# An edge-gated graph layer on one core: the weighted copy of a part taken over into the next part, and the hot edges' W2 products put ahead of the hot tiles' products

## The chip, the core and the metric

The kernel runs on one core of a Trainium2 chip. The metric is device time in microseconds (us), the median of several executions. One further execution was taken with the hardware profiler; all rows of a profile come from it. The engines are called TensorE (PE in the rows; PEld is its weight load), VectorE (DVE), ScalarE (ACT), GpSimd (POOL) and SyncE (SP, which issues DMAs here).

## The reference

There are 12,500 nodes with 128 features and 412,500 edges (each drawn edge in both directions, and a loop for each node), sorted by destination. All is float32.

```
theta = x[dst] - x[src]
w     = sigmoid(relu(theta @ W1 + b1) @ W2 + b2)          # one number per edge
agg   = segment_sum(w * theta, dst)
indeg = segment_sum(1, dst)
out   = layernorm(x + agg + indeg * (x @ W4 + b4))
```

## The kernel before, in words

**Preparation.** A table z is written to DRAM that holds for each node the rows `x @ W1` and x side by side, so that one gather by source brings both. The first 18 parts (`PLAIN`) are handled by `early_part`, which the change doesn't touch.

**Parts and blocks.** The other edges are cut into parts of 1532 consecutive edges (`CE`). Two parts make a block of destinations (`SUB = 2`): an even part (h = 0) begins the block b, an odd one (h = 1) ends it. `part(s)` (L1459) writes down the work of one part in the program's order, for s from 18 up to the last part and a few beyond. TensorE, VectorE and ScalarE are under a manual schedule: each runs its instructions in the order in which `part` calls them. What one engine needs from another is waited for by semaphores that the framework inserts.

**Ordinary edges.** Up to 1024 edges of a part are gathered, 128 by each of eight indirect DMAs on GpSimd (`gather`, L398), three parts ahead. TensorE spreads the destinations' rows to the edges by one-hot products (`spread_y`, L885, two parts ahead, into one of two PSUM banks called y). VectorE subtracts the gathered rows (L943), applies relu and W2 (L948), sums to the logits `lg` (L954) and compares indices to make the one-hots `ow` (`one_hot_w`, L918); L918 comes ahead of L954 in even parts and behind it in odd ones. ScalarE makes the gate, a sigmoid of `lg`: once into the PSUM tile `fix` (`open_gate`, L960) and once into the row buffer `wx` (`gate_sums`, L966). Then the gathered x rows are multiplied by the gate into `wx`: four of the eight slots by VectorE (`weigh`, L988, the weighted copy), four by ScalarE (`weigh_rest`, L995). In the next part TensorE sums `wx` by destination (`begin_block` in an odd part, `add_block` in an even one, both L1130).

**Hot edges.** Up to 512 other edges of a part (`HK`) have sources in small ranges of nodes that are kept on chip (`tabs`), so they are not gathered but fetched by one-hot products. ScalarE makes the one-hots `of` of one set of tiles in a part (`hot_tiles` L1033 and L1035, called by `fetch_step` at the end of a part), TensorE multiplies in the next part (`products_of_tiles`, `hot_products`, L1049, 16 products), and ScalarE copies the result to `xT` in the part after that (`hot_out`, L1063). One part ahead of their sums, the hot edges of part t = s + 1 go through `hot_turned` (L1076 and L1077, into the bank `pz`), `hot_relu` (ScalarE, L1082), `hot_rows` (L1090: the W2 products, four of them, into `fix`; L1093: four transposes of xT into `pz`) and `hot_weights` (ScalarE: L1099 sigmoid, L1102 four weighted evictions of `pz`). `one_hot_h` (VectorE, L1112) makes their destinations' one-hots `owh` once a block, in the even part.

**The shared bank.** `fix` is one PSUM bank that holds an index row (read by L918 and L1112), W2 (read by L948), the hot edges' logits (written by L1090, read by L1099), the gates (written by L960, read by L988) and the block's own rows (`own`, written by L1205, read and written by L1223).

**Ends of blocks.** In an odd part the block before is ended: `total` (L1184), `finish` (L1195), `own` (L1203, L1205), and on VectorE `normalize` (L1223 to L1248). `shift` (L1124, L1125) makes the matrix that carries sums over from block to block.

**Placing of the edge lists.** A generator `place` sorts the next 64 parts' edge lists into hot and ordinary slots, mainly on VectorE (32 rounds of L576, L580, L583 a list, and others) with some steps on ScalarE and TensorE. It is advanced in small steps by `spend`, which has a credit of 2.5 a part, so that a part holds about 3 us of it until a list is done. There are five lists; the last four are placed during the stage of `part`.

Of the kernel before, what the change touches and what calls it, by code (L numbers as in the profile page):

```python
# [44 lines left out]
PLAIN = FIRST + MORE  # L45
# [37 lines left out]
def gnn_resnorm(  # L83
# [41 lines left out]
    NS = PLAIN - (E1 - E) // CE  # L125
    NF = PLAIN + (E - E1) // CE
    TAIL = E - E1 - (NF - PLAIN) * CE
    NK = NS // SUB
# [9 lines left out]
    while n0 < N:  # L138
        t = max(1, (N - n0) // P)
# [231 lines left out]
    def filled(t, s):  # L371

        if s < NF:
            return t
        return t.rearrange("p (h j) d -> p h j d", h=2)[:, :, :JT, :]

    def wx_of(s):

        if s < NH:
            return wxe_buf[s % 2]  # L380
        return wx_buf[s % (EW if s < PLAIN else NW)]

    def rows_of(s):

        if s < NH:
            t = zbuf[s // 2].rearrange("p k d -> p (k d)")[:, (s % 2) * BE:(s % 2 + 1) * BE]
            return t.rearrange("p (k d) -> p k d", d=D)
        return zbuf[(s - NH + NX) % NZ]
# [322 lines left out]
    with tc.manual_schedule(engines={SP}), tc.tile_pool(name="work", bufs=2) as wp, tc.tile_pool(  # L711
# [143 lines left out]
        def one_hot(b, c0=0, c1=RW):  # L855

            at = (b - PLAIN // SUB) % NO * RW
            oh = oh_all[:, at:at + RW]
            blocks[b]["oh"] = oh
            if not c0:  # L860
                for i in range(SUB):
                    parts[b * SUB + i] = {"oh": oh}
            oh = oh[:, c0:c1]
            nc.scalar.activation(oh, blocks[b]["to_all"][:, c0:c1], AF.Abs, scale=mine, bias=away)
            nc.scalar.activation(oh, oh, AF.Relu, scale=-1.0, bias=1.0)  # L865
# [106 lines left out]
        def weigh(s):  # L972

            zs = rows_of(s)
            if s < PLAIN:
                wx = wx_of(s)
                for k in range(K):
                    nc.scalar.activation(wx[:, k, :D], zs[:, k, :] if s < NH else zs[:, k, D:],
                                         AF.Copy, scale=wx[:, k, D:D + 1])
                return  # L980
            w = gate[:, s % 2].rearrange("p (k e) -> p k e", e=1)
            wx = wx_of(s)[:, :, :D]
            if s < NF:
                xs = zs[:, :KV, D:]
                w, wx = w[:, :KV], wx[:, :KV]
            else:
                xs, w, wx = filled(zs[:, :, D:], s), filled(w, s), filled(wx, s)
            nc.vector.tensor_tensor(wx, xs, w.to_broadcast(list(xs.shape)), op=OP.mult)  # L988

        def weigh_rest(s):  # L990

            if s < NF:
                wx = wx_of(s)
                for k in range(KV, K):
                    nc.scalar.activation(wx[:, k, :D], rows_of(s)[:, k, D:], AF.Copy,  # L995
                                         scale=wx[:, k, D:D + 1])
# [87 lines left out]
        def hot_rows(t):  # L1084

            xT = xT_all[:, (t - PLAIN) % HX, :]
            hr = parts[t]["hr"]
            for q in range(HQ):
                at = slice(q * P, (q + 1) * P)
                nc.tensor.matmul(lgh[:, t % SUB, q:q + 1], hr[:, at], w2_c, start=True, stop=True)  # L1090
            for q in range(HQ):
                at = slice(q * P, (q + 1) * P)
                newest[0] = nc.tensor.transpose(pz[:, at], xT[:, at], ident)  # L1093

        def hot_weights(t):

            b, h = divmod(t, SUB)
            wx = wxh_buf[b % len(wxh_buf)][:, h * HQ:(h + 1) * HQ, :]
            nc.scalar.activation(wx[:, :, D:D + 1], lgh[:, h].rearrange("p (q e) -> p q e", e=1),  # L1099
                                 AF.Sigmoid, bias=b2_c)  # L1100
            for q in range(HQ):
                nc.scalar.activation(wx[:, q, :D], pz[:, q * P:(q + 1) * P], AF.Copy,  # L1102
                                     scale=wx[:, q, D:D + 1])
# [13 lines left out]
        def shift(b):  # L1117

            sh = blocks[b]["sh"] = wp.tile([P, WB], F32, name="sh")
            if b * SUB < PLAIN:  # L1120
                nc.vector.tensor_scalar(sh[:WB, :WB], lag[:WB, :WB], step_c[:WB, b:b + 1],
                                        None, op0=OP.is_equal)
                return
            nc.scalar.activation(sh[:WB, :WB], lag[:WB, :WB], AF.Abs, scale=-1.0, bias=step_c[:WB, b:b + 1])  # L1124
            nc.scalar.activation(sh[:WB, :WB], sh[:WB, :WB], AF.Relu, scale=-1.0, bias=1.0)  # L1125
# [71 lines left out]
        def own(b):  # L1197

            d = blocks[b]
            a = d["a"]  # L1200
            plain = b * SUB < PLAIN
            sw = wp.tile([P, 2], F32, name="sw")
            nc.scalar.activation(sw[:WB], a[:WB, D:AW], AF.Copy, bias=1.0)  # L1203
            d["own"] = d["xw"][:WB] if plain else own_f[:WB]
            nc.scalar.activation(d["own"], d["xw"][:WB], AF.Copy, scale=sw[:WB, 0:1])  # L1205
            d["deg"] = a[:WB, D + 1:AW] if plain else sw[:WB, 1:]
# [45 lines left out]
        def fetch(b):  # L1252
            if b < NK:
                load_block(b)
# [32 lines left out]
        def advance(kinds, n=1):  # L1287

            for _ in range(n):
                if steps[0] is None or steps[1] not in kinds:  # L1290
                    return
                steps[1] = next(steps[0], None)
                if steps[1] is None:
                    steps[0] = None
# [8 lines left out]
        def tiles_of(group):  # L1303

            x = 0
            for f in group:
                hot_tiles(f, x)
                tiled.append((f, x))
                x += (f[2] - f[0]) * EP
# [9 lines left out]
        def fetch_step(s):  # L1319

            for f in rest_of:
                if f[0] - 4 == s:
                    tiles_of([f])
# [4 lines left out]
        def spend(kinds, most=NS):  # L1328

            while most and credit[0] > 0 and steps[0] is not None and steps[1] in kinds:  # L1330
                credit[0] -= cost[steps[1]]
                advance(kinds)
                most -= 1
# [117 lines left out]
        def spread_ahead(s):  # L1451

            if s + 2 < NS:
                spread_y(s + 2)
                if PLAIN + AHEAD <= s + 3 < NS:
                    paced[s + 3] = newest[0]
                    gather(s + 3)

        def part(s):  # L1459

            b, h = divmod(s, SUB)
            t = s + 1
            credit[0] = min(credit[0] + 2.5, 5.0)
            if s in turns:
                edges[s + 3] = turns[s], load(turns[s])
            if s in edges:
                i, loaded = edges.pop(s)
                assert steps[0] is None
                steps[:] = place(i, lambda: where[0](), *loaded), "k"
            for f in rest_of:  # L1470
                if f[0] - 7 == s:
                    hot_load(f)
            if h == 0:
                fetch(b + 2)
            if s == PLAIN:
                normalize(b - 2)
            done_b = h == 1 and PLAIN // SUB - 1 <= b - 1 < NK
            if t < NS:
                hot_turned(t)
            while opened:  # L1480
                hot_out(*opened.pop(0))
            if t < NS:
                hot_relu(t)
            if done_b:
                total(b - 1)
            advance("c")
            if s < NS:
                logits(s)
            if done_b:
                finish(b - 1)  # L1490
            spread_ahead(s)
            if tiled:
                products_of_tiles()
            if t < NS:
                hot_rows(t)
            if h == 0 and PLAIN // SUB <= b - 1 < NK:
                add_block(b - 1)
            if h == 1 and b < NK:
                begin_block(b)
            if h == 0 and b + 1 < NK:  # L1500
                one_hot(b + 1, BP, RW)
            if h == 1 and b + 2 < NK:
                one_hot(b + 2, 0, BP)
            if t < NS:
                hot_weights(t)
            if s < NS:
                open_gate(s)
                if h == 0:
                    one_hot_h(b)
                else:  # L1510
                    shift(b)
                    spend("kz", 1)
                weigh(s)
                gate_sums(s)
            if done_b:
                own(b - 1)
            if s < NS:
                weigh_rest(s)
            spend("kspmz")
            if done_b:  # L1520
                normalize(b - 1)
            fetch_step(s)

        with tc.manual_schedule(engines=IN_ORDER):
            for s in range(PLAIN, NS + 4):
# [201 lines left out]
```

## Time and profile before

| | us |
|---|---|
| median of 3 executions | 3545.08 (3541.45 to 3546.11) |
| the profiled execution | 3547.81 |
| its span, first to last instruction | 3545.8 |
| stage of `part`, from the first L943 to the last | 302.2 to 3522.5 |
| busy TensorE, weight loads | 2803.1 (79%), 2335.3 (66%) |
| busy VectorE | 2421.4 (68%) |
| busy ScalarE | 2427.3 (68%) |
| busy GpSimd | 2143.9 (60%) |
| mean granted TensorE clock | 0.883 of full |

How to read the rows: in the order of time a row gives its start, its length, engine, line, operation, `out<-in`, shapes and, in square brackets, how long the engine sat idle ahead of it and what ended that. In the windows a row gives the stretch, its length, the busy time of the engines with their instructions in brackets, the granted TensorE clock, the DMA share and GB/s. In the waits a row gives the waiting engine and line, what it waited for, total us, times and the longest. An engine that waits costs time only if it is on the chain that sets the end of a part.

### The profile page before, as it was taken

To read this page: it belongs to the slowest core of one execution; us is meant where nothing else is said; L and a number is where in the kernel's file an instruction comes from. 1 tells how busy PE (TensorE), PEld (TensorE's weight loads), DVE (VectorE), ACT (ScalarE), POOL (GpSimd) and SP (SyncE) were. 2 spreads that over 40 slices of the span, in tenths; PEclk is the share of its full clock that TensorE was granted. 3 is DMA by queue.
4 is the path that set the end of the run, shared out by engine and by line. 5 is a ranking of instruction groups with operands and counts; after the bars stand their busy time and mean duration, and the time that the engine had idled before them with its cause. 6 is when DMAs were issued, how large, how long until landed. Compare 5 with 4: busy or idle time off the path is not lost.

```text
span 3545.8 us, 53797 instructions
## 1 busy us (share of the span) xinstructions
PE 2803.1 (79%) x16422; PEld 2335.3 (66%) x16422; DVE 2421.4 (68%) x4015; ACT 2427.3 (68%) x6397; POOL 2143.9 (60%) x2213
## 2 busy tenths in 40 slices
PE   6777887777787788877887877877887877877787
PEld 5666666666666666666776666656776666666675
DVE  7996676776656777766556767766656766766655
ACT  5357767676677676766786676766786676666775
POOL 3756566665566666655575665655576666655663
PEclk7769899998999899998898999989898989988998
DMA  7545344343444343433353444433444434434442
GB/s 259 170 114 133 108 109 113 109 116 104 110 123 114 108 115 109 115 109 107 108 145 107 110 112 109 117 103 107 116 132 110 110 105 113 117 100 104 112 121 60
DMA packets 239302, 413.24 MB, mean 117 GB/s; under 512 B 63423, under 2 KB 147226, under 8 KB 237470
## 3 DMA queue, kind: packets, MB, share of 16 engines
q0 software_dynamic: 105280, 286.93, 29.0%
q1 hardware_dynamic: 131756, 116.40, 12.7%
q10 hardware_dynamic: 1970, 6.40, 0.5%
q8 instruction: 133, 2.18, 0.3%
q14 instruction: 163, 1.34, 0.1%
HBM read 388.57 MB, written 20.94 MB: 115 GB/s over the span
## 4 chain that ended last, share of the span: by engine, by line
PE 33%; DVE 25%; ACT 16%; issue 11%; DMA 7%; POOL 7%; DVEq 0%; ACTq 0%; SPq 0%; POOLq 0%
PE pd L1049 13%; POOL zbuf L398 7%; PE y L885 6%; ACT wxh L1102 5%; DMA zbuf<-z,src_i 5%; DVE zbuf L943 5%; PE fix L1090 5%; PE pa L1130 4%; PE pz L1093 3%; DVE wx L988 3%; DVE ed L580 2%; DVE owh L1112 2%; DVE ew L583 2%; ACT of L1033 2%; DVE ew L576 2%
## 5 line engine op out<-in xcount | busy, mean ns | idle before, releaser
L398 POOL DMA_INDIRECT zbuf<-z,src_i x2060 | 1994.0, 968 | 1252.7 <-PE pa L1130 659.3
L885 PEld LDWEIGHTS y<-y,oh 128*128 128x128 f32 (+1 forms) x2108 | 314.4, 227 | 804.4 <-DVE zbuf L943 778.1
L885 PE MATMUL y<-y,oh 128*128 128x128 f32 (+1 forms) x2108 | 366.9, 328 | 601.9 <-DVE zbuf L943 595.1
L1049 PE MATMUL pd<-of,tabs 128*128 128x128 f32 (+2 forms) x4240 | 710.6, 339 | 21.2 <-ACT xT L1063 21.1
L1049 PEld LDWEIGHTS pd<-of,tabs 128*128 128x128 f32 x4240 | 686.9, 254 | 29.4 <-ACT xT L1063 29.3
L1099 ACT ACTIVATE wxh<-fix,b_c 128x4 f32<-128x4 f32 x258 | 69.0, 267 | 803.9 <-PE fix L1090 801.1
L1130 PE MATMUL pa<-wx,ow 128*104 128x260 f32 (+1 forms) x2284 | 533.4, 379 | 0.0
L1112 DVE TENSOR_TENSOR owh<-fix,hrel 128x832 f32<-128x832 f32 x129 | 132.2, 1025 | 552.8 <-ACT fix L960 552.8
L988 DVE TENSOR_TENSOR wx<-zbuf,fix 128x512 f32<-128x512 f32 x258 | 176.5, 684 | 407.0 <-ACT fix L960 407.0
L1130 PEld LDWEIGHTS pa<-wx,ow 128*104 128x104 f32 x2284 | 368.5, 176 | 78.3 <-issue 0.9
L1102 ACT ACTIVATE wxh<-pz,wxh 128x128 f32<-128x128 f32 x1032 | 294.6, 368 | 78.3 <-PE pz L1093 76.8
L1033 ACT ACTIVATE of<-hot_src,nodes 128x512 f32<-128x512 f16 (+2 forms) x530 | 343.5, 695 | 2.4 <-PE pd L1049 2.4
L948 DVE SCALAR_TENSOR_TENSOR zbuf<-zbuf,fix 128x1024 f32<-128x1024 f32 x273 | 331.6, 1215 | 13.4 <-ACT wxh L1099 4.1
L954 DVE TENSOR_REDUCE lg<-zbuf 128x8 f32<-128x1024 f32 x273 | 329.8, 1208 | 5.0
L995 ACT ACTIVATE wx<-zbuf,wx 128x128 f32<-128x128 f32 x1028 | 326.6, 388 | 0.0
L943 DVE TENSOR_TENSOR zbuf<-y,zbuf 128x1024 f32<-128x1024 f32 x258 | 314.6, 1219 | 9.1 <-issue 6.6
L1090 PEld LDWEIGHTS fix<-w_c,hr 128*128 128x128 f32 x2064 | 274.1, 207 | 16.5 <-issue 16.1
L1035 ACT ACTIVATE of<-of 128x1024 f32<-128x1024 f32 (+1 forms) x265 | 274.1, 1035 | 8.3
L1090 PE MATMUL fix<-w_c,hr 128*128 128x1 f32 x2064 | 264.2, 249 | 11.5 <-DVE ow L918 11.2
L1076 PE MATMUL pz<-xT,wni 128*128 128x512 f32 x516 | 266.0, 598 | 2.4 <-ACT wxh L1102 2.4
L1077 PE MATMUL pz<-oh,y 128*128 128x512 f32 x516 | 266.3, 598 | 0.2 <-ACT oh L865 0.2
L1130 PE MATMUL pa<-wxh,owh 128*104 128x130 f32 x2064 | 260.8, 281 | 0.0
(302 smaller groups left out, 4167.6 us busy)
## 6 DMA issues: line engine op xcount, KB each, us to landing
to_all<-off_d SPq DMA_DIRECT2D x258, 128.0 KB
zbuf<-z,src_i POOLq DMA_INDIRECT x2060
hot_src<-hot_s SPq DMA_DIRECT2D x228, 128.0 KB
z<-zbuf SPq DMA_DIRECT2D x10, 1024.0 KB
y<-z SPq DMA_DIRECT2D x270, 28.0 KB
xw<-in_x_dram SPq DMA_DIRECT2D x138, 52.0 KB
out_dram<-o SPq DMA_DIRECT2D x138, 52.0 KB
wx<-in_x_dram ACTq DMA_DIRECT2D x12, 512.0 KB
```

The source lines that it names most:

```text
L398: ins = nc.gpsimd.indirect_dma_start(out=rows_of(s)[:, k, :], out_offset=None, in_=z if s >= NH else x, in_offset=IndirectOffsetOnAxis(ap= ...
L885: nc.tensor.matmul(y[:, j, :], d["oh"][:, (k0 + j) * P:(k0 + j + 1) * P], y_of(s), start=True, stop=True)
L943: nc.vector.tensor_sub(half, yy.to_broadcast([P, 2, n, D]), half)
L948: nc.vector.scalar_tensor_tensor(h[:, at, :], h[:, at, :], 0.0, w2.to_broadcast([P, n, D]), op0=OP.max, op1=OP.mult)
L954: nc.vector.tensor_reduce(lg[:, at, 0], h[:, at, :], AX.X, OP.add)
L988: nc.vector.tensor_tensor(wx, xs, w.to_broadcast(list(xs.shape)), op=OP.mult)
L995: nc.scalar.activation(wx[:, k, :D], rows_of(s)[:, k, D:], AF.Copy, scale=wx[:, k, D:D + 1])
L1033: nc.scalar.activation(of[:, t, :], hot_src[:, i % NU, :w], AF.Abs, bias=nodes[:, t:t + 1])
L1049: newest[0] = nc.tensor.matmul(to[:, q], tabs[:, g * RG + q, t, :], of[:, t, q], start=t == 0, stop=t == HT - 1)
L1090: nc.tensor.matmul(lgh[:, t % SUB, q:q + 1], hr[:, at], w2_c, start=True, stop=True)
L1102: nc.scalar.activation(wx[:, q, :D], pz[:, q * P:(q + 1) * P], AF.Copy, scale=wx[:, q, D:D + 1])
L1130: newest[0] = nc.tensor.matmul(to if len(w.shape) == 3 else to[:, 0, :], one, w, start=first and i == 0, stop=last and i == len(terms) - 1)
```

## The change

The instructions stay the same; their order within `part` changes. (1) `weigh` of a part is called in the next part, ahead of `logits`. (2) `hot_rows`, the W2 products and transposes, come ahead of `products_of_tiles`. (3) `shift` comes ahead of `hot_weights`. (4) `own` comes ahead of `open_gate`. (5) The one placing step that stood ahead of `weigh` in odd parts is left to the later `spend`. (6) `fetch_step` comes ahead of that `spend` and of `normalize`.

```diff
@@ part(s)
             advance("c")
+            if PLAIN < s <= NS:
+                weigh(s - 1)
             if s < NS:
                 logits(s)
             if done_b:
                 finish(b - 1)
             spread_ahead(s)
+            if t < NS:
+                hot_rows(t)
             if tiled:
                 products_of_tiles()
-            if t < NS:
-                hot_rows(t)
             if h == 0 and PLAIN // SUB <= b - 1 < NK:
                 add_block(b - 1)
...
             if h == 1 and b + 2 < NK:
                 one_hot(b + 2, 0, BP)
+            if h == 1 and b < NK:
+                shift(b)
             if t < NS:
                 hot_weights(t)
+            if done_b:
+                own(b - 1)
             if s < NS:
                 open_gate(s)
                 if h == 0:
                     one_hot_h(b)
-                else:
-                    shift(b)
-                    spend("kz", 1)
-                weigh(s)
                 gate_sums(s)
-            if done_b:
-                own(b - 1)
-            if s < NS:
                 weigh_rest(s)
+            fetch_step(s)
             spend("kspmz")
             if done_b:
                 normalize(b - 1)
-            fetch_step(s)
```

## The prediction

> **What bounds the kernel now.** I read the page first, then the list of waits, then the order of time of one odd and one even part engine by engine, and at last the windows, for the clock. On the page no engine is busy all the time, so the bound is a chain that hands the work round. The waits name it (engine, line, who is waited for, total us, times, longest):
>
> ```profile
> ACT wxh L1099 <- PE fix L1090: 801.1, 255, 9.0
> ...
> PE y L885 <- DVE zbuf L943: 595.1, 220, 8.6
> DVE owh L1112 <- ACT fix L960: 552.8, 129, 7.8
> POOL zbuf L398 <- issue: 483.1, 1563, 5.2
> DVE wx L988 <- ACT fix L960: 407.0, 127, 5.4
> ...
> PE fix L1090 <- DVE ow L918: 11.2, 26, 7.4
> ```
>
> TensorE waits for VectorE's subtraction L943 (it frees the y bank), and VectorE waits for ScalarE's gate L960, 960 us in all. VectorE in an odd part (h = 1, begun by the L943 at 2032.40) and the even part after it:
>
> ```profile
> 2032.40 1.23 DVE L943 TENSOR_TENSOR zbuf<-y,zbuf 128x1024 f32<-128x1024 f32 x1 [0.20 <-issue]
> ...
> 2036.05 0.58 DVE L918 TENSOR_TENSOR ow<-fix,rel 128x416 f32<-128x416 f32 x1
> ...
> 2040.96 0.69 DVE L988 TENSOR_TENSOR wx<-zbuf,fix 128x512 f32<-128x512 f32 x1 [3.21 <-ACT fix L960]
> ...
> 2043.63 0.29 DVE L1223 TENSOR_TENSOR fix<-fix,a 104x128 f32<-104x128 f32 x1
> ...
> 2045.04 1.23 DVE L943 TENSOR_TENSOR zbuf<-y,zbuf 128x1024 f32<-128x1024 f32 x1
> ...
> 2047.44 0.58 DVE L918 TENSOR_TENSOR ow<-fix,rel 128x416 f32<-128x416 f32 x1
> ...
> 2051.98 1.02 DVE L1112 TENSOR_TENSOR owh<-fix,hrel 128x832 f32<-128x832 f32 x1 [2.83 <-ACT fix L960]
> ...
> 2056.97 1.23 DVE L943 TENSOR_TENSOR zbuf<-y,zbuf 128x1024 f32<-128x1024 f32 x1 [0.20 <-issue]
> ```
>
> The odd part takes 12.64 us, of which VectorE idles 3.21; the even one 11.93, with 2.83 idle. VectorE's own work is therefore 9.43 and 9.10. The gate it waits for stands in ScalarE's order behind the weights of the hot edges, which wait for the W2 products L1090; those stand in TensorE's order behind the tiles' products L1049:
>
> ```profile
> 2033.68 1.16 PE L885 MATMUL y<-y,oh 128*128 128x128 f32 x8 [2.23 <-DVE zbuf L943]
> 2034.67 3.29 PE L1049 MATMUL pd<-of,tabs 128*128 128x128 f32 x16
> 2037.75 1.28 PE L1090 MATMUL fix<-w_c,hr 128*128 128x1 f32 x8
> ...
> 2047.32 1.95 PE L1049 MATMUL pd<-of,tabs 128*128 128x128 f32 x16
> 2049.10 0.95 PE L1090 MATMUL fix<-w_c,hr 128*128 128x1 f32 x8
> ```
>
> So the loop is L943, y 1.28 us later, tiles 0.99 after that, W2 products 1.78 (even) or 3.08 (odd) later, gate, VectorE's rest, next L943. The same 16 products take 1.78 or 3.08 because of the clock, the third number of this window from inside the odd tiles:
>
> ```profile
> 2036.20:2037.80 1.60, 1.60 (x10) 0.50 0.30 92
> ```
>
> The half clock comes right behind the 2.23 us in which TensorE stood still.
>
> **The change, part by part.** Nothing is added to or taken from the work; six steps change place.
>
> *W2 products and transposes ahead of the tiles.* This takes the tiles (1.78 at full clock) off the way to the gate. But the W2 products write the bank `fix`, which L918 reads, and the last wait quoted shows that they wait for L918. In an odd part L918 ends at 36.05 + 0.58 - 32.40 = 4.23 us after L943, in an even one at 47.44 + 0.58 - 45.04 = 2.98. Apart from one of 7.4 us the 26 waits come to 11.2 - 7.4 = 3.8, 0.15 us each, the handing over from L918's end; I add that. So the new W2 products start at 4.38 (odd) and 3.13 (even) instead of 37.75 - 32.40 = 5.35 and 49.10 - 45.04 = 4.06. Behind the waiting product stand, in TensorE's order, the transposes, the tiles, the block's sums, the next pz products and the next y; ScalarE's hot weights and gate wait for them. y ends at 1.28 + 0.99 = 2.27, so TensorE now stands still for 2.1 us (odd) and 0.9 us (even) in the middle of a part, where it did not.
>
> *Even part.* From the W2 products to the one-hot L1112, which waits for the gate, pass 51.98 - 49.10 = 2.88 us. Gate for VectorE: 3.13 + 2.88 = 6.01. VectorE is there at 51.98 - 2.83 - 45.04 = 4.11, so its wait falls from 2.83 to 1.90 and the part from 11.93 to **11.0**. The weighted copy, now at the head of the next part, costs its time either way.
>
> *Odd part.* Here `own` moves ahead of the gate and `shift` ahead of the hot weights, where ScalarE waits for the W2 products anyway (the first wait quoted, 801 us in all). `own` costs what lies between L1203 and L995:
>
> ```profile
> 2041.74 0.19 ACT L1203 ACTIVATE sw<-a 104x2 f32<-104x2 f32 x1
> 2041.96 0.37 ACT L1205 ACTIVATE fix<-xw,sw 104x128 f32<-104x128 f32 x1
> 2042.27 1.26 ACT L995 ACTIVATE wx<-zbuf,wx 128x128 f32<-128x128 f32 x4
> 2043.44 1.32 ACT L1033 ACTIVATE of<-hot_src,nodes 128x512 f32<-128x512 f16 x2
> 2044.79 1.06 ACT L1035 ACTIVATE of<-of 128x1024 f32<-128x1024 f32 x1
> ```
>
> that is 0.53. Gate: 4.38 + 2.88 + 0.53 = 7.79. Nothing of VectorE needs it now until the normalizing (1.41 us from L1223 to L943): the placing steps that stood behind the weighted copy fill the wait. Ahead of the normalizing and the copy (0.6 with its gap) VectorE has 9.43 - 1.41 - 0.6 = 7.42 us of work; L1223 writes `fix` behind the gate, so it starts at 7.79, 0.37 late. The part becomes 9.43 + 0.37 = **9.8** instead of 12.64. The copy does most of this, not the swap: with the copy in its old place, ahead of two placing steps and the normalizing, 45.04 - 40.96 = 4.08 us would still follow the gate, 11.9 in all.
>
> *Tiles' one-hots (fetch_step) ahead of the placing.* ScalarE's placing steps (list loading only) come 1.32 + 1.06 = 2.4 us later; VectorE waits for a few of them. Bounds: 0, or four lists times three steps times 2.4 = 29 us. I take 15. SyncE's loads of `hot_src` wait for L1033, which comes no later than now, so that queue is not hurt; the gathers on GpSimd still wait for the last product of the block's sums, which remains the last of TensorE's part.
>
> *What is late next.* The pair of parts is 9.8 + 11.0 = 20.8 us for VectorE, against 24.57. TensorE at full clock, in a pair without placing work:
>
> ```profile
> 1797.20:1816.90 19.70, 17.80 (x118) 14.60 (x118) 11.98 (x19) 16.94 (x47) 14.83 (x17) 1.00 0.53 140
> ```
>
> 17.8 busy (first number behind the length), and with the new gaps of 2.1 and 0.9 it comes to 20.8 as well; ScalarE has 16.9. GpSimd:
>
> ```profile
> L398 POOL DMA_INDIRECT zbuf<-z,src_i x2060 | 1994.0, 968 | 1252.7 <-PE pa L1130 659.3 <-issue 453.2 <-ACT src_i L705 25.4
> ```
>
> 16 gathers of 0.968 and 0.31 between them (483.1 / 1563) are 20.4 a pair, or 10.2 a part. Four engines end within 4 us of each other; the gain stops there.
>
> *Clock.* If the half clock follows the new 2.1 us gap as it follows the 2.23 us one, tiles and W2 products take 1.30 + 0.33 = 1.63 longer in that pair. Only the W2 share reaches the gate at once; the rest makes the next y late. Ends 0 and 1.63; I take 1.0, in half of the pairs, since the pair at 1797 went through a gap of 1.66 us at clock 1.00. The pair becomes **21.3**. The Trainium skill, page "TensorE: Matmul & The Clock Gate", section "What's actually happening", says that the clock is halved after an idle window of about 3.4 us; by that rule neither new gap would trip it and the pair would stay at 20.8. The trace disagrees: here 2.23 us were followed by 0.50.
>
> *The sum*, against the profiled execution's own 3547.81 us (2 us of it outside the span). The L943 row counts the parts:
>
> ```profile
> L943 DVE TENSOR_TENSOR zbuf<-y,zbuf x258: 685/1225/1226, 302.2 to 3522.5; 128x1024 f32<-128x1024 f32 x129
> ```
>
> 257 intervals in 3220.3 us. Counted in VectorE's order of time, 199 of them hold placing work (2581.7 us, 12.97 each) and 58 none (638.6 us, 11.0 each). The 199 are longer than the 12.29 of the quoted pair; I scale them: 12.97 x 21.3 / 24.57 = 11.24, saving 1.73 each, 344 us. The 58 can fall at most to the gathers' 10.2; I take half of that, 0.4 each, 23 us. Less 15 for the list loading: 352. 3547.8 - 352 = 3196; the median of the shown runs is 2.7 below this execution: about **3190**.
>
> **The rivals.**
> - *The clock stays full.* 12.97 x 20.8 / 24.57 = 10.98, saving 1.99 x 199 = 396, with 23 and -15: 3140. For it: less standing still in all. Against it: the 2.23 us gap above. The rule of the Trainium skill named above (page "TensorE: Matmul & The Clock Gate") would lead here.
> - *The gathers become the bound and all else fits under them*: 257 x 10.2 = 2621 instead of 3220: 2950. Against it: VectorE's 20.8 a pair lies above 20.4.
> - *The one-hot wait eats the swap.* If both gaps halve the clock, a pair takes 20.8 + 2 x 1.0 to 2 x 1.63, 22.8 to 24.1, and 199 parts save 0.93 to 0.25 each; 3360 to 3495, say 3430. For it: L918 ends at a fixed distance from L943 and TensorE can fill the gap with nothing, since the tiles are queued behind it. The change may also not do what it says, since the copy still stands in the loop, directly ahead of L943: if only the even part's 0.9 is saved, 129 times, that is 116 us, 3430 again.
> - *Slower.* The mechanism is the same gap with a clock that stays down: at half clock each us loses half a us of TensorE work, and TensorE has 20.8 of 24.57 to itself. It decides when the pair loses over 3.8 us, 7.6 us at half clock of 24.6, a granted clock below 0.85. Over the stage it is now 0.90:
>
> ```profile
> 302.00:3522.00 3220.00, 2576.80 (x15187) 2138.81 (x15186) 2154.06 (x3437) 2263.71 (x6012) 1972.54 (x2038) 0.90 0.41 112
> ```
>
> At 0.80 the pair would be about 25.8, 0.6 us a part more: 3700. Against it: y's waits of 595.1 / 220 = 2.7 us, two in a pair, give way to 2.1 + 0.9 = 3.0.
>
> **How the numbers follow.** Forecast 0.60 (3190, its own range 3110 to 3290); full clock 0.13; gathers 0.05; one-hot wait 0.12; no change 0.03; slower 0.07. A difference under 0.2% can't be told from none here. Faster 0.90, same 0.03, slower 0.07. The range leaves out the gathers' floor, the upper two thirds of the one-hot case and the slower one: 3060 to 3350.
>
> **What would show it.** L1112's wait falls by about a third and L988's (now at the head of a part) nearly vanishes; L1223 has a short wait for L960; L1090 waits for L918 in almost every part, about 2 us in odd and 0.9 in even ones; y's wait for L943 shrinks; GpSimd's share rises. Wrong would be: VectorE still idle 3 us a part, a clock well under 0.90, or gathers that L943 waits for.

## The result, and the profile after

| | before | after |
|---|---|---|
| median of 4 executions each, us | 3543.26 (3538.79 to 3546.11) | 3240.93 (3227.77 to 3246.97) |
| ratio after / before | | 0.9143 [0.911, 0.9175] |
| profiled execution, span, us | 3547.81, 3545.8 | 3245.33, 3243.3 |
| stage of `part`, first to last L943, us | 3220.3 | 2919.3 |
| mean granted clock over the span | 0.883 | 0.880 |

The change saves 8.6%, 302 us. 301 of the profile's 302.5 come out of the stage of `part`. The forecast was 3190, 51 us too low, inside its range.

The page of the changed kernel: all four engines have the busy time that they had, within 30 us, in 302 us less.

```profile
span 3243.3 us, 53854 instructions
...
PE 2793.9 (86%) x16422; PEld 2346.8 (72%) x16422; DVE 2413.1 (74%) x4015; ACT 2456.1 (76%) x6397; POOL 2163.7 (67%) x2213
```

The list of waits of the changed kernel, in the columns of before's:

```profile
DVE owh L1112 <- ACT fix L960: 398.8, 126, 7.8
...
ACT hr L1082 <- PE pz L1077: 286.8, 197, 5.5
...
DVE fix L1223 <- ACT fix L960: 211.2, 115, 4.9
PE fix L1090 <- DVE ow L918: 197.7, 121, 7.4
ACT wxh L1099 <- PE fix L1090: 196.1, 102, 5.5
...
PE y L885 <- DVE zbuf L943: 108.1, 60, 10.1
```

L988's wait of 407 us for the gate has left the list. L1112's fell from 552.8 to 398.8, TensorE's for L943 from 595.1 to 108.1, ScalarE's for the W2 products from 801.1 to 196.1. Three are new or grown, each for something that used to be ready in time: L1090 for L918, L1223 for the gate, and ScalarE's L1082 for the products of `pz`, whose place in the order is the old one, but to which TensorE now comes later than ScalarE.

VectorE in the order of time, one odd part (9.94 us, L943 to L943) and the even part after it (10.72), at full clock:

```profile
2701.68 1.22 DVE L943 TENSOR_TENSOR zbuf<-y,zbuf 128x1024 f32<-128x1024 f32 x1
...
2709.64 0.30 DVE L1223 TENSOR_TENSOR fix<-fix,a 104x128 f32<-104x128 f32 x1 [0.42 <-ACT fix L960]
...
2711.02 0.68 DVE L988 TENSOR_TENSOR wx<-zbuf,fix 128x512 f32<-128x512 f32 x1
2711.62 1.22 DVE L943 TENSOR_TENSOR zbuf<-y,zbuf 128x1024 f32<-128x1024 f32 x1
...
2717.69 1.02 DVE L1112 TENSOR_TENSOR owh<-fix,hrel 128x832 f32<-128x832 f32 x1 [1.97 <-ACT fix L960]
...
2722.34 1.22 DVE L943 TENSOR_TENSOR zbuf<-y,zbuf 128x1024 f32<-128x1024 f32 x1
```

What to see: the odd part has 0.42 us of waiting left where it had 3.21, the even one 1.97 where it had 2.83; the copy L988 stands directly ahead of L943 and waits for nothing. TensorE, the W2 products of the even part ahead and then this odd part:

```profile
2694.08 1.02 PE L1090 MATMUL fix<-w_c,hr 128*128 128x1 f32 x8 [0.61 <-DVE ow L918]
...
2702.96 1.16 PE L885 MATMUL y<-y,oh 128*128 128x128 f32 x8
2706.05 1.02 PE L1090 MATMUL fix<-w_c,hr 128*128 128x1 f32 x8 [1.94 <-DVE ow L918]
...
2707.41 1.95 PE L1049 MATMUL pd<-of,tabs 128*128 128x128 f32 x16
```

The W2 products wait for L918, 0.61 us in the even part and 1.94 in the odd one; y waits for nothing. Here the tiles run at full speed, 1.95 us. In other pairs they don't, and a pair is longer; the windows of the changed kernel, a pair at full clock and one that is partly at half:

```profile
2691.00:2711.60 20.60, 17.95 (x119) 14.66 (x118) 17.80 (x28) 17.05 (x47) 15.78 (x16) 1.00 0.52 137
1852.90:1875.30 22.40, 20.36 (x118) 17.28 (x117) 17.82 (x29) 17.14 (x47) 16.09 (x16) 0.86 0.46 120
```

The quoted pair is among the short ones. Of the 69 pairs of a regular odd part and a regular even part behind it ("regular" is explained with the table), 8 ran at full clock throughout, with a median of 20.66 us; the mean of all 69 is 22.44.

The part lengths, counted in VectorE's order of time from one L943 to the next (us, means). "Regular" parts hold 2.5 to 3.4 us of placing work, the 46 others more or less than that, four of them a loading of a list:

| | 76 regular even | 77 regular odd | 58 without placing | 46 others |
|---|---|---|---|---|
| before | 12.98 | 12.52 | 11.01 | 13.72 |
| after | 11.81 | 10.64 | 10.36 | 13.07 |
| swap only (first experiment) | 11.37 | 12.06 | 10.11 | 13.43 |
| all but the swap (second experiment) | 12.49 | 10.52 | 10.68 | 12.71 |

### The profile page after: what moved, and what is told of

Its sections match the earlier page's. It is cut to its first block, busy times and chain, and to the rows that moved or that the text cites. A ratio compares the mean times of both kernels' runs of the same rounds, so it can differ in the third digit from the quotient of the medians.

```text
span 3243.3 us, 53854 instructions
## 1 busy us (share of the span) xinstructions
PE 2793.9 (86%) x16422; PEld 2346.8 (72%) x16422; DVE 2413.1 (74%) x4015; ACT 2456.1 (76%) x6397; POOL 2163.7 (67%) x2213
## 3 DMA queue, kind: packets, MB, share of 16 engines
q14 instruction: 165, 1.35, 0.1%
## 4 chain that ended last, share of the span: by engine, by line
## 5 line engine op out<-in xcount | busy, mean ns | idle before, releaser
L1049 PE MATMUL pd<-of,tabs 128*128 128x128 f32 (+2 forms) x4240 | 666.8, 325 | 0.0
L1049 PEld LDWEIGHTS pd<-of,tabs 128*128 128x128 f32 x4240 | 649.7, 242 | 0.0
L1130 PE MATMUL pa<-wx,ow 128*104 128x260 f32 (+1 forms) x2284 | 542.9, 384 | 1.8 <-DVE wx L988 1.8
L1090 PE MATMUL fix<-w_c,hr 128*128 128x1 f32 x2064 | 308.1, 270 | 226.9 <-DVE ow L918 197.7
L885 PEld LDWEIGHTS y<-y,oh 128*128 128x128 f32 (+1 forms) x2108 | 274.7, 196 | 283.4 <-DVE zbuf L943 215.3
L1090 PEld LDWEIGHTS fix<-w_c,hr 128*128 128x128 f32 x2064 | 294.6, 220 | 253.1 <-ACT sh L1125 103.0
L1112 DVE TENSOR_TENSOR owh<-fix,hrel 128x832 f32<-128x832 f32 x129 | 132.2, 1025 | 410.5 <-ACT fix L960 398.8
L885 PE MATMUL y<-y,oh 128*128 128x128 f32 (+1 forms) x2108 | 299.1, 286 | 118.6 <-DVE zbuf L943 108.1
L1082 ACT ACTIVATE hr<-pz 128x512 f32<-128x512 f32 x258 | 154.0, 597 | 286.9 <-PE pz L1077 286.8
L1033 ACT ACTIVATE of<-hot_src,nodes 128x512 f32<-128x512 f16 (+2 forms) x530 | 343.9, 696 | 3.5 <-PE pd L1049 2.4
L943 DVE TENSOR_TENSOR zbuf<-y,zbuf 128x1024 f32<-128x1024 f32 x258 | 313.6, 1216 | 0.0
L1130 PEld LDWEIGHTS pa<-wxh,owh 128*104 128x104 f32 x2064 | 248.0, 175 | 0.0
```

The lines of the kernel that those rows point to most:

```text
L885: nc.tensor.matmul(y[:, j, :], d["oh"][:, (k0 + j) * P:(k0 + j + 1) * P], y_of(s), start=True, stop=True)
L943: nc.vector.tensor_sub(half, yy.to_broadcast([P, 2, n, D]), half)
L1033: nc.scalar.activation(of[:, t, :], hot_src[:, i % NU, :w], AF.Abs, bias=nodes[:, t:t + 1])
L1049: newest[0] = nc.tensor.matmul(to[:, q], tabs[:, g * RG + q, t, :], of[:, t, q], start=t == 0, stop=t == HT - 1)
L1130: newest[0] = nc.tensor.matmul(to if len(w.shape) == 3 else to[:, 0, :], one, w, start=first and i == 0, stop=last and i == len(terms) - 1)
```

## The experiments

The theory: the two main edits work on different parts, the swap on the even one and the copy's place on the odd one; what was missing from the forecast went to the clock and to the loading of lists. The rivals: one edit does it all; the wait of L1090 for L918 is what costs; TensorE's work is the bound and the clock doesn't matter. Every kernel was timed beside the kernel before on the same chip. There were three chips, on which the kernel before took 3544, 4060 and 4098 us; times of these are compared by their ratios alone. The chip of the result above is not on record; the kernel before took 3543 us there, so its 3240.93 us are set beside the times of the first chip.

### The swap alone (first chip, before 3544.31)

```diff
 (before)    spread_ahead(s)
-            if tiled:
-                products_of_tiles()
             if t < NS:
                 hot_rows(t)
+            if tiled:
+                products_of_tiles()
```

> The kernel before with one edit: the W2 products and transposes ahead of the tiles' products; the weighted copy, own, shift and fetch_step stay where they were. My theory (the swap shortens the even part, the copy's place the odd one): gate at 6.01 us in an even part, which becomes 11.0; in an odd part the gate comes at 4.38 + 2.88 = 7.26 and the copy, two placing steps and the normalizing (4.08) still follow it, 11.3; 22.3 a pair at full clock against 24.57, with half-clock stretches 22.3 to 23.3: about 3375 us, 3340 to 3420. Rival (the copy's place is of no account, the swap does it all): 3240. Rival (the wait for the one-hot eats the swap): 3500 or more.

Measured: 3323.37 us, 0.9383 [0.9363, 0.9404]. That is below the theory's 3340 to 3420, and near neither rival. VectorE's order of time in this kernel, an odd part's L988 and the two of the next pair:

```profile
2703.91 0.69 DVE L988 TENSOR_TENSOR wx<-zbuf,fix 128x512 f32<-128x512 f32 x1 [2.14 <-ACT fix L960]
...
2714.15 1.02 DVE L1112 TENSOR_TENSOR owh<-fix,hrel 128x832 f32<-128x832 f32 x1 [1.97 <-ACT fix L960]
...
2726.42 0.69 DVE L988 TENSOR_TENSOR wx<-zbuf,fix 128x512 f32<-128x512 f32 x1 [1.97 <-ACT fix L960]
```

The even part's wait is 1.97 as in the changed kernel, so the swap alone shortens the even part. It also takes 1.1 to 1.2 us off the odd part's wait (3.21 before): in the odd part quoted before, the tiles ran at half speed, and the swap takes them off the way to the gate. Odd parts shrink less on the mean (12.52 to 12.06), even ones more (12.98 to 11.37).

### The change without the swap (first chip)

```diff
 (after)     spread_ahead(s)
-            if t < NS:
-                hot_rows(t)
             if tiled:
                 products_of_tiles()
+            if t < NS:
+                hot_rows(t)
```

The steps of `own`, `shift`, `fetch_step` and the placing are in this kernel too; no run took the copy's place apart from them.

> The changed kernel with the swap undone: tiles' products ahead of the W2 products as before, while the weighted copy stands at the head of the next part, with own, shift and fetch_step as in the change. My theory: the even part stays at 11.93 (the one-hot L1112 still waits for the late gate); in the odd part the gate comes at 5.35 + 2.88 + 0.53 = 8.8 against 7.4 us of VectorE's own work, so it becomes about 10.8 instead of 12.64; 22.7 a pair: about 3340 us, 3300 to 3390. L1090 hardly waits for L918. Rival (the copy moved stands in the loop all the same): 3540. Rival (the copy's place does it all): 3240.

Measured: 3281.81 us, 0.9261 [0.9243, 0.9279]. That is below the theory's 3300 to 3390, and near neither rival. VectorE's order of time, odd part and even part, and TensorE's W2 products of that odd part:

```profile
2695.42 1.22 DVE L943 TENSOR_TENSOR zbuf<-y,zbuf 128x1024 f32<-128x1024 f32 x1
...
2705.36 1.22 DVE L943 TENSOR_TENSOR zbuf<-y,zbuf 128x1024 f32<-128x1024 f32 x1
...
2712.57 1.02 DVE L1112 TENSOR_TENSOR owh<-fix,hrel 128x832 f32<-128x832 f32 x1 [3.11 <-ACT fix L960]
...
2717.22 1.22 DVE L943 TENSOR_TENSOR zbuf<-y,zbuf 128x1024 f32<-128x1024 f32 x1
```

```profile
2699.80 1.02 PE L1090 MATMUL fix<-w_c,hr 128*128 128x1 f32 x8 [0.15 <-DVE ow L918]
```

The odd part is 9.94 us without the swap, and the even one 11.86, with a wait no shorter than the old 2.83. The W2 products of the odd part start 2699.80 - 2695.42 = 4.38 us after L943, as early as with the swap: at full clock the tiles are done by the time L918 is, so there the swap has nothing left to take. The two save 221 and 262 us alone and 302 together. They don't add in either kind of part. By the table the regular odd parts lose 0.46 and 2.00 us alone and 1.88 together, the even ones 1.61 and 0.49 alone and 1.17 together. In odd parts both take the same time at half speed. In even parts the clock may be why, which is higher here than with the swap; what it is worth was not measured. The windows of this kernel, and below it those of the changed one:

```profile
302.00:3100.00 2798.00, 2329.61 (x14316) 1898.29 (x14315) 2050.22 (x3302) 2154.55 (x5663) 1883.55 (x1933) 0.94 0.45 122
```

```profile
302.00:3100.00 2798.00, 2459.22 (x14578) 2059.83 (x14578) 2078.05 (x3341) 2207.91 (x5772) 1925.70 (x1968) 0.90 0.46 125
```

0.94 against 0.90 (the third number from the end), though TensorE stands still longer in the kernel with the higher clock: it waits 414.2 us for L943, where the changed kernel waits 108.1. From this kernel's waits:

```profile
DVE owh L1112 <- ACT fix L960: 498.2, 126, 9.4
...
PE y L885 <- DVE zbuf L943: 414.2, 219, 11.0
```

The last section comes back to that.

### The tiles' one-hots last again (first chip)

```diff
                 weigh_rest(s)
-            fetch_step(s)
             spend("kspmz")
             if done_b:
                 normalize(b - 1)
+            fetch_step(s)
```

> The changed kernel with fetch_step (ScalarE's one-hots of the tiles) back behind the placing steps and the normalizing. My theory: the four list loadings, whose longest parts went from 17.6, 14.9, 17.6 and 17.6 us to 21.0, 18.2, 23.2 and 22.4 with the change, get back to about 17 each, since VectorE no longer waits for ScalarE's list steps behind 2.4 us of one-hots: 15 to 25 us less, 3215 to 3230. The square roots with their table loads also come ahead of the one-hots again. Rival (the early fetch_step pays elsewhere, by starting the next part's ScalarE work earlier): 3245 to 3290.

Measured: 3225.87 us, 0.91 [0.908, 0.9119]. That is inside the theory's range and 15 us under the changed kernel, but the two intervals overlap. The four parts in which a list is loaded took 67.7 us in sum before the change, 84.8 after it (17.6, 14.9, 17.6, 17.6 became 21.0, 18.2, 23.2, 22.4) and 74.0 here, so this edit gives back 10.8 of them, not all as expected. In VectorE's order of time of the changed kernel one such part has

```profile
1709.87 0.15 DVE L535 TENSOR_SCALAR et<-et 128x1 f32<-128x1 f32 x1 [6.75 <-ACT et L530]
```

and ScalarE in the same part does the tiles' one-hots first:

```profile
1706.60 1.32 ACT L1033 ACTIVATE of<-hot_src,nodes 128x512 f32<-128x512 f16 x2
1707.95 1.06 ACT L1035 ACTIVATE of<-of 128x1024 f32<-128x1024 f32 x1
1708.91 0.92 ACT L530 ACTIVATE et<-ed,col 128x766 f32<-128x766 int32 x1
```

### Odd parts with the tiles first (first chip)

```diff
             spread_ahead(s)
+            if tiled and h == 1:
+                products_of_tiles()
             if t < NS:
                 hot_rows(t)
```

(In this kernel `products_of_tiles` leaves nothing for its later place in odd parts.)

> The changed kernel, but in odd parts the tiles' products come ahead of the W2 products again; even parts keep the swap. In an odd part L918 lets the W2 products start at 4.38 us at the earliest, and y with the tiles at full clock ends at 2.27 + 1.78 = 4.05, so the tiles fill the gap. My theory: the gate comes no later and TensorE no longer stands still for 2.1 us there, so the half clock is rarer and TensorE's pair is 2 us shorter: pairs of 20.6 or a little less everywhere instead of a mean of 22.4, 3100 to 3170 us. Rival (odd tiles run at half clock as they did before the change and put the gate at 8.8): the odd part 10.8 and more, 3230 to 3300.

Measured: 3263.23 us, 0.9219 [0.9196, 0.9241]. The theory fell: the long gap of the odd part is gone, but half speed moved into the even parts. About 100 of the 256 groups of tiles run at half speed in both kernels; in the changed kernel some 80 of them lie in odd parts, here all but two in even ones. TensorE's order of time, an even part that begins with y at 2651.71:

```profile
2651.71 1.16 PE L885 MATMUL y<-y,oh 128*128 128x128 f32 x8 [1.44 <-DVE zbuf L943]
2653.56 1.78 PE L1090 MATMUL fix<-w_c,hr 128*128 128x1 f32 x8 [0.69 <-DVE ow L918]
...
2656.09 3.62 PE L1049 MATMUL pd<-of,tabs 128*128 128x128 f32 x16
```

The size is the rival's, but not its reason, since the odd parts stayed as long as they were (10.54 us against 10.64).

### The gap filled with extra products (second and third chip)

Odd parts do the 16 products of the tiles once more, ahead of `hot_rows`: 1.78 us of TensorE work at full clock where it waited 1.94.

```diff
             spread_ahead(s)
+            if h == 1:
+                bank = None
+                for f, x in tiled:
+                    bank, _ = hot_products(f, x, bank)
             if t < NS:
                 hot_rows(t)
```

> The changed kernel with work added: in odd parts TensorE does the 16 tiles' products once more, into the same bank, ahead of the W2 products, where it waits for L918; the proper ones follow in their place and overwrite them. Nothing else moves. 129 x 1.78 us of TensorE work are added. Theory (the half clock that follows the gap is what separates the mean pair of 22.4 us from the full-clock pair of 20.65): the gap is filled, the tiles' groups at half clock fall from 100 to under 50, pairs stay near 20.7, and the kernel with more work is faster: 3130 to 3210 us. Rival (TensorE's work is the bound, not its clock): 3300 to 3470. Rival (neither): 3241.

Measured on the second chip (before 4059.97): 4055.57 us, 0.9984 [0.9962, 1.0006]. The changed kernel had not been timed there, so it was run with the changed kernel on the third chip (before 4098.5).

> The changed kernel itself, beside the three below on one chip. The four runs before these came from a chip on which the kernel before takes 4060 us instead of 3544 and TensorE and ScalarE show waits (issue, remote) that the other profiles lack, so they can't be set against the changed kernel's 3241. Theory: 0.914 of the kernel before where that takes 3544; on a chip with late transfers a ratio nearer to 0.93, since waits for transfers are added to both.

> The changed kernel with the odd parts' 16 tiles' products done twice, once in the gap ahead of the W2 products. Clock theory: at or below the changed kernel run beside it, since tiles' groups at half clock fall from 100 to under 50 and that outweighs 129 x 1.78 us of added TensorE work laid into a gap of 2.1. Rival (TensorE's work binds): 3 to 7% above it. On the stalling chip it came to 0.998 of the kernel before, with 123 of 338 groups at half clock, which speaks for the rival.

Measured there: the changed kernel 3770.19 us, 0.9187 [0.9165, 0.9209]; with the gap filled 4161.06, 1.016 [1.0134, 1.0186]. The filling costs 391 us, 3.0 us for each of the 129 odd parts, and the clock hardly moves (0.843 and 0.858 over the spans, and some 130 groups of tiles at half speed in both). But two things keep this from being a test of the clock. First, the gap was hardly there: on this chip the changed kernel waits for L918 for 42.1 us in all, not 197.7 (row below, in the next experiment). Second, the filling brought a wait of ScalarE with it. In the 77 regular odd parts the W2 products start 4.37 us after L943 and end at 5.39 in both kernels (medians), but their sigmoid L1099 starts at 5.84 in the changed kernel and at 9.26 in the filled one. From the waits of the changed kernel on the third chip, and then of the filled one:

```profile
ACT wxh L1099 <- PE fix L1090: 28.7, 36, 3.4
```

```profile
ACT wxh L1099 <- PE pd L1049: 427.3, 92, 7.0
...
ACT wxh L1099 <- remote: 338.1, 62, 7.1
```

L1099 reads `fix` and a constant, and why it waits for tile products that stand behind the W2 products is open. So this run decides neither for the clock theory nor for its rival.

### The index row from SBUF (second and third chip)

L918 reads the index row from its SBUF copy instead of the bank `fix`, so that L1090 need not wait for it:

```diff
+    iota_s = iota_row[:, :WB].rearrange("p (o m) -> p o m", o=1)
...
-                    ow[:, :n], iota_f.to_broadcast([P, n, WB]),
+                    ow[:, :n], iota_s.to_broadcast([P, n, WB]),
```

> The changed kernel, but L918 reads its index row from the SBUF copy of it instead of the bank fix, so that the W2 products wait in that bank only for L948, which ends 2.47 us after L943. Theory (the new wait for L918 is what the swap pays): W2 products at about 2.6 instead of 3.1 and 4.4; odd gate at 6.0, ahead of VectorE's own work, odd part 9.5; even gate at 5.5, even part 10.5; 20.0 a pair at full clock, the gathers' 20.4 if they bind, fewer half-clock stretches: 3090 to 3170 us. Rival (the wait costs nothing because TensorE has to wait for the next y anyway): 3225 to 3250. Rival (the SBUF operand makes L918 itself slower): its 0.58 us rises.

> The changed kernel with L918 reading the SBUF copy of the index row. Theory (the new wait for L918 is what the swap pays): 2 to 4% below the changed kernel run beside it. Rival (TensorE would wait for the next y or for hr instead): within 0.7% of it. The wait of L1090 for L918 (198 us) must be gone in both cases.

Measured: second chip 3692.06 us, 0.91 [0.9077, 0.9123]; third chip 3737.84, 0.9126 [0.9104, 0.9149], 0.7% below the changed kernel by the ratios, whose intervals lie just apart. The theory's 2 to 4% did not come; the rival's 0.7% did. (One line is added, so L1091 here is L1090 there.) The waits of the changed kernel on the third chip, and then of this one:

```profile
ACT of L1033 <- remote: 440.4, 162, 4.5
...
PE fix L1090 <- ACT hr L1082: 166.2, 63, 4.0
...
PE fix L1090 <- DVE ow L918: 42.1, 39, 7.4
```

```profile
PE fix L1091 <- ACT hr L1083: 205.0, 74, 4.1
...
PE fix L1091 <- ACT xT L1064: 119.9, 34, 5.7
```

The wait for L918 is gone (on this chip it was only 42.1 us in the changed kernel), and the W2 products wait for ScalarE's relu and copies instead. L918 itself takes 584 ns from SBUF against 581 from PSUM. So on this chip the wait for L918 is worth little: it is short, and the next input is late too. What its removal is worth on the first chip, where it came to 197.7 us, was not run.

The same for L1112 as well, `owh` from SBUF (second chip):

```diff
-                d["owh"], iota_f.to_broadcast([P, n, WB]),
+                d["owh"], iota_s.to_broadcast([P, n, WB]),
```

> As the run before it, and the block's one-hot L1112 reads the SBUF copy too, so that it waits for no gate. Theory: the 399 us of L1112's wait vanish; the even part falls to VectorE's own 9.1 or to what the gathers (10.2 a part) and TensorE allow; 20.4 a pair or a little more: 3040 to 3130 us. Rival (another wait takes its place at once, ScalarE's hr for the pz products or the weighted copy for the gate): within 20 us of the run before it.

Measured: 3647.3 us, 0.8983 [0.8961, 0.9006], 1.3% below the kernel with L918 alone by the ratios, a gain between the theory's and the rival's. With `fetch_step` last besides, as in the third experiment (second and third chip):

> As the run before it, with fetch_step back at the end of the part. Theory: the list loadings again gain 15 us as in the run with that edit alone; 10 to 20 us below the run before it. Rival: with VectorE nearer to its bound ScalarE's one-hots come too late for the tiles, no gain or a loss.

> The changed kernel with L918 and L1112 reading the SBUF copy and fetch_step at the end of the part. Theory: the 399 us of L1112's wait for the gate vanish, pairs come near to the gathers' 20.4 and the list loadings gain 15 us: 4 to 6% below the changed kernel run beside it, 3050 to 3110 us where the kernel before takes 3544. Rival (the waits return at the weighted copy and at the next y): less than 2% below it.

Measured: second chip 3575.43 us, 0.8801 [0.8773, 0.8828]; third chip 3638.66, 0.8861 [0.8838, 0.8883], 3.5% below the changed kernel there, less than the theory's 4 to 6%. On the second chip the step back of `fetch_step` gave 72 us where 10 to 20 were expected; the four parts with a loading account for 22 of them (105.5 to 83.7), and the rest is open. It is the fastest version that was run on these two chips. It was not run on the first, so how it stands there to 3225.87 is open. The waits of this kernel on the third chip: L1112 no longer waits for the gate, and what is late next is again ScalarE's relu.

```profile
PE fix L1091 <- ACT hr L1083: 345.0, 107, 6.4
DVE a L1196 <- ACT hr L1083: 329.3, 87, 4.6
```

## Why the prediction was right, and where its sizes were off

**What bounds the kernel.** Right: the loop through W2 products, gate and VectorE. All the time came out of it, with no work taken away.

**Even part, 11.93 to 11.0.** 10.72 at full clock. L1112's wait is 1.97 where 1.90 was worked out. The swap alone gives the same wait, the change without it none shorter than the old: shown.

**Odd part, 12.64 to 9.8.** 9.94. L1223 waits 0.42 where 0.37 was worked out, L1090 waits 1.94 where it was 2.1. The change without the swap gives 9.94 too: shown, and so is that the swap isn't what makes the odd part short. That it is the copy's place rather than `own`, `shift` and the placing step, which moved with it, is argued from VectorE's order: the copy's wait of 3.21 is what went.

**The tiles' one-hots, +15.** +17.1, the four parts' 84.8 - 67.7. Putting the step back gives 10.8 of it.

**The pair at full clock, 20.8.** 9.94 + 10.72 = 20.66.

**The clock, +1.0 in half of the pairs.** This is the term that was too small, in size and in number. The pair quoted above with part of it at half speed took 22.40 us, 1.8 more than the 20.60 of the one at full clock and more than the upper end of 1.63. And about 100 of the 256 groups of tiles ran at half speed, nearly all in different ones of the 128 pairs, where one in every second pair was taken. The 69 regular pairs took 22.44 on the mean, 1.8 over the 20.66 at full clock, where the term gave 0.5. The scaling hid most of that: before the change these pairs took 25.53 on the mean, not the 24.57 of the quoted one, so the scaled forecast for them was 22.13. The premise, half speed behind a long gap of TensorE, also fails in the very stretch that was quoted. The y of the even part there waited still longer:

```profile
2046.32 1.16 PE L885 MATMUL y<-y,oh 128*128 128x128 f32 x8 [2.91 <-DVE zbuf L943]
```

The tiles behind it (the row at 2047.32) took 1.95 us, full speed. So the length of the gap alone doesn't decide; the last section goes on from here.

**The sum.** It promised 344 us from the 199 parts with placing work, 23 from the 58 without, and -15. Measured: 263.5 from the 199 with the loss of 17.1 in them, so 280.6 without; 37.5 from the 58 (10.36 where 10.6 was forecast). The 14 us that the 58 gave beyond a guessed half made the miss smaller by luck. The missing 63 us of the 199 are 26 in the 153 regular ones, which saved 1.53 us each where the scaled forecast was 1.70, and 37 in the 46 others. The scaling is the step that failed for those: it lets a part save in proportion to its length, but a part that is longer because it holds more placing work has no more idle time to lose. That reason is argued from the lengths; the 46 were not taken apart.

**The rivals.** *Full clock*: no, 0.90 in the stage, as before. *Gathers as the floor*: no, L943 waits for no gather; but the parts without placing work come within 0.2 us of it. With the swap alone they took 10.11 on the mean, so the 10.2 that was worked out is no floor. *The one-hot wait eats the swap*: partly, as the clock. *Slower*: the clock did not stay down.

**What would show it.** Right: L1112's wait down by 28%, L988's gone, L1223's short one, y's smaller one, GpSimd's share up from 60 to 67%. Wrong: that L1090 waits for L918 in almost every part. It did 121 times, 92 of them in odd parts (1.94 us, and 0.61 in an even one); in even parts that follow a stretch of half speed, y itself comes late and L918 is done by then. So the W2 products of the regular even parts start 3.98 us after L943 (median), not 3.13.

## What to carry to other kernels

When a chain goes round several engines, work out for each wait what would be late next before pricing its removal: here the swap and the rest of the change, worth 221 and 262 us alone, gave 302, since the time that one takes is in part the time that the other takes. A third edit, which took away TensorE's wait for L918, gave under 1% on a chip where that wait was only 42 us in all. A part with a wait is best filled with work that is there anyway (the placing steps), by moving what needs the late value to the other side of it. And look at what stands directly behind a gap of TensorE: by the counts below, products of one column there can prolong the gap as far as the clock is concerned.

## What the runs showed of the hardware

**The clock is set on a fixed grid of 3.41 us.** In eight of the traces (before, after, the first four experiments, and the two of the third chip with and without the filled gap) every stretch of one granted clock is a multiple of 3.413 us long and all changes lie on one grid. So each grid stretch can be held against the speed of the next. Windows of the changed kernel on that grid, over an odd part that fell to half speed and one that did not (busy TensorE is the first number behind the length, the clock the third from the end):

```profile
1865.70:1869.11 3.41, 1.47 (x12) 1.31 (x12) 3.38 (x6) 2.82 (x7) 2.50 (x4) 1.00 0.36 102
1869.11:1872.52 3.41, 3.41 (x18) 3.41 (x18) 2.72 (x4) 1.44 (x6) 2.80 (x3) 0.50 0.34 91
1872.52:1875.94 3.42, 3.42 (x17) 3.28 (x16) 2.51 (x7) 3.36 (x11) 2.18 (x3) 0.50 0.38 116
1875.94:1879.35 3.41, 3.41 (x14) 2.11 (x14) 3.38 (x4) 1.82 (x5) 1.27 (x2) 1.00 0.42 97
...
2701.96:2705.37 3.41, 2.06 (x11) 1.04 (x9) 3.34 (x4) 2.44 (x6) 2.49 (x4) 1.00 0.45 135
2705.37:2708.79 3.42, 2.73 (x25) 2.77 (x26) 3.35 (x7) 1.86 (x8) 2.81 (x3) 1.00 0.38 108
2708.79:2712.20 3.41, 3.41 (x20) 2.57 (x19) 2.85 (x9) 3.35 (x12) 2.50 (x4) 1.00 0.35 91
```

The same stretches, with L1090 (the W2 products) alone:

```profile
1865.70:1869.11 3.41, 0.35 (x4) 0.38 (x4) 1.00 0.36 102
1869.11:1872.52 3.41, 1.19 (x7) 1.10 (x6) 0.50 0.34 91
```

Both odd parts have the same wait of 1.94 us. In the first it lies whole in one grid stretch, which is left with 1.47 us of work (1.12 without the W2 products), and the next one runs at half speed. In the second it is cut in two by the grid, 2.06 and 2.73 are left (2.06 and 1.71 without them), and nothing happens. The stretch at 1869.11 is busy throughout and yet the speed doesn't come back behind it, but behind the next: 1.19 of its 3.41 us are W2 products, of one column each. The next one has none.

Counting without the W2 products makes the rule sharp. The grid stretches of the stage in these eight traces (the bounds of the rows were chosen by these same counts):

| work of TensorE in a grid stretch | next one at half speed, W2 products left out | the same, W2 products counted |
|---|---|---|
| at full speed, under 1.3 us | 691 of 692 | 402 of 402 |
| at full speed, 1.3 to 1.8 | 276 of 566 | 449 of 598 |
| at full speed, 1.8 or more | 6 of 4453 | 122 of 4711 |
| at half speed, under 2.5 | 549 of 550 | 231 of 231 |
| at half speed, 2.5 to 3.0 | 30 of 165 | 90 of 112 |
| at half speed, 3.0 or more | 14 of 851 | 272 of 1223 |

At the same total the difference stays. Of the stretches at full speed with 1.8 to 2.5 us of work, 80 of 96 are followed by half speed where 0.8 us or more of it are W2 products, and 5 of 462 where under 0.1 us are. At half speed with 3.0 us or more, half speed stays in 259 of 275 against 15 of 748.

So in this kernel about 1.5 us of work in 3.41 decides going down, and some 2.5 to 3 coming back, and the W2 products hardly count as work. The puzzles fit this: the prediction's gap of 1.66 us at clock 1.00 (it leaves 1.75), the 2.23 us followed by 0.50 (1.35 are left), the 2.91 followed by full speed (the grid cuts it, 1.55 and 2.36 are left), and the share of stretches at half speed is 188 of 932 before, 105 of 855 with all but the swap, but 177 of 843 after and 181 of 866 with the swap alone: the swap puts 1.02 us of W2 products directly behind the gap of 1.94. That the one-column shape is the reason is read from these counts; no run changed the shape or put other products behind the gap. The rival of full clock went by the Trainium skill, page "TensorE: Matmul & The Clock Gate", section "What's actually happening": it gives a free-running window of 3413 ns, and the grid here agrees with that; it has the clock fall after an idle window, and here a window with up to about 1.5 us of work does it.

**Chips differ.** On the second and third chip the same kernel before took 15 and 16% longer than on the first, and the granted clock over the span was about 0.85 where it was 0.88 to 0.89. Their profiles show waits that are put down to no engine ("remote"), ScalarE's L1033 for instance 440 us in the changed kernel on the third chip. The cause was not settled; the ratio of the change is the same there, 0.9187 [0.9165, 0.9209] against 0.9143 [0.911, 0.9175].
